# Moving four feature sums, and three products that read them, within layer four of a graph network

## The chip, the cores and the metric

The kernel runs on one core of a Trainium2 chip. Its time is the device time of one launch in microseconds (us). A core has five engines that run their own queues of instructions in order, and wait for one another by semaphores: TensorE (in the profile PE; its weight loads PEld) multiplies matrices into PSUM, VectorE (DVE) and ScalarE (ACT) work element by element, GpSimd (POOL) does so more slowly, and SyncE (SP) issues the DMAs that move data between HBM and SBUF.

## The reference, cut to what matters

There are 16 graphs, each with 1024 nodes of 128 features and a dense 1024 x 1024 adjacency. First comes a small graph network with a layer norm, then a network of four layers with a layer norm:

```
x = layernorm(x + L0(x, adj))          # one aggregation over adj, one linear map, relu
x = layernorm(x + L1(x, adj))          # four layers:
def _layer(nodes, adj, ...):
    src_agg = einsum('bjv,bij->biv', nodes @ ws + bs, l2norm(adj, 2))
    dst_agg = einsum('bjv,bji->biv', nodes @ wd + bd, l2norm(adj, 1))
    self_rep = nodes @ wn + bn
    return tanh(concatenate([src_agg, self_rep, dst_agg]) @ wu + bu)
```

Layers one and two read the output of the layer before. Layers three and four read it together with earlier outputs: layer four reads the outputs of layers three, two and the network's input, 384 features a node. Everything is float32.

## The kernel before, in words

**Folding.** The matrices of a layer are folded, so that a layer is: messages (a linear map of the node features, one part for each direction of the adjacency, SRC and DST), the product of the messages with the scaled adjacency `a` and its scaled transpose `at`, an own part (a linear map of the node's own features), and tanh. Features lie with the feature on the partitions: `f1T` (layer one's output), `f23T` (layer two's, later layer three's), `x_T` (the network's input, also called x1T).

**Seven products instead of eight.** The product of messages and adjacency is done as a 2 x 2 block product in the manner of Strassen and Winograd, so that it takes seven products of quarters. VectorE makes the sums of messages that this needs, S2 to S4 (lines 660 to 663), and the sums of quarters of the adjacency, T2 to T4 for `a` and Q2 to Q4 for `at` (helper `combine`, lines 628 to 632). The products are called M1, M2, M3, M4, Z11, Z12 and Z21; M1 to M4 go to PSUM banks of their own (A, Bk, Dk, Ck), and the Z ones straight to the output halves Z0 and Z1. In layers three and four the own part is done in the same way with the same seven names: its "quarters" are the halves of two feature tensors, in layer four `f1T` and `x_T`. The sums of these quarters are `feature_sums`, four subtractions on VectorE (L798 to L801); in layer four they are made in place. Three of the own products, M1, Z11 and Z12, read the features as they were before; M2, M3, M4 and Z21 read the sums.

**Steps.** A product of 128 x 64 weights fills half of TensorE's columns, so two of them run at once: `upper` and `lower` are two lists of products, and `in_turn` issues them alternately. A step is one entry of `upper` beside one of `lower`, each in two passes; the own product of M3 is cut into two halves of half a step. In layer four there are 34 steps. All engines but SyncE run in the order in which the program is written; SyncE's order comes from the compiler's scheduler. What other engines do during a layer is placed by step: `events` (inside `aggregate`: the sums, and the reads of PSUM, `m1_read` to `last_reads`) and `hooks` (work for other graphs) are dictionaries from an upper step to a function, which is called ahead of that step; at one step the event goes ahead of the hook.

**What lies around the change.** While layer four of graph b runs, the hooks do the first layer norm of graph n = b + 1 and prepare its adjacency:

- step 0, `squares0`: the sum v of squares (L400)
- step 7, `rstd0`: a small product pv on TensorE, ve from it on VectorE (L408), the power -1/2 on GpSimd (L410, output rs), and then `combine(4)`, the subtraction L632 that makes the quarter sum T4 of graph b again (`T_again`), since the first network of graph n had used its place
- step 14, `end0`: the features times rs (L415), and their transposes into the place of `x_T` (L450)
- step 18, `quarters0`: T2 and T3 of graph n (L628, L630); steps 23 and 27: the transposes of its rows into `at` (L605), from row loads (`rows`, `rows_xa`, `rows_acc`) that ScalarE has scaled (L597)

Then layer one of graph n begins: its messages (L206), the additions of the bias to them (L648), their sums S (L660 to L663), and its 30 steps. Its hook at step 0 makes the last transposes, from `rows`, `rows_xa` and `rows_acc`. This is so for 15 of the graphs; the last has no next one.

Of the kernel before, what the change touches and what calls it, by code (L numbers as in the profile page):

```python
# [23 lines left out]
def adj_resnorm_kernel(ctx: ExitStack, tc: tile.TileContext, x, adj, w0, b0, layers, out):  # L24
# [44 lines left out]
    NJ = NB // 2  # L69

    def blocks(ap):

        return ap.rearrange("p (k g c) -> p g k c", g=G, c=C)
# [5 lines left out]
    def half(h):  # L79
        return slice(h * HW, (h + 1) * HW)  # L80
# [127 lines left out]
    def product(name, i=None):  # L208
        if i is None:
            return ps_t.tile([P, HW], F32, tag="pt", name=name)  # L210
        return ps_p.tile([P, HW], F32, tag=f"p{i}", name=name)
# [422 lines left out]
    SRC, DST = 0, 1  # L634
# [58 lines left out]
    def aggregate(b, l, feats, msgs, wm, a, at, T, Q, fT, etag, hooks={}, pieces=1, sums=None):  # L693
# [5 lines left out]
        Z0, Z1 = (product(f"z{h}_{l}_{b}", h) for h in range(NH))  # L699

        Ck = product(f"m4_{l}_{b}")
        Dk = product(f"m3_{l}_{b}")
        A, Bk = (product(f"m{i}_{l}_{b}") for i in (1, 2))
# [4 lines left out]
        def own(v, h, chosen=feats):  # L708
            return [(own_weights(wm, l, c)[:, v * V:(v + 1) * V], blocks(f[:, half(h)])) for f, c in chosen]

        def prod(name, part):
            y, t = Y[part], TT[part]
            x, y = {"M1": lambda: (X[0, 0], y[0, 0]), "M2": lambda: (S[2], t[2]), "M3": lambda: (S[3], t[3]),
                    "M4": lambda: (S[1], y[0, 1]), "Z11": lambda: (X[0, 1], y[1, 0]),
                    "Z12": lambda: (S[4], y[1, 1]), "Z21": lambda: (X[1, 1], t[4])}[name]()
            return [(x[:, k, part], y[:, k]) for k in range(NJ)]
# [3 lines left out]
        def m1_read():  # L720
            nc.scalar.copy(e0[high], A[high])  # L721
            nc.scalar.copy(e0[low], A[high])

        def m4_read():
            nc.scalar.copy(e2[high], Ck[low])
            nc.scalar.copy(e2[low], Ck[low])
# [15 lines left out]
        def m3_half():  # L742
            nc.scalar.copy(e1[high], Dk[low])

        def m2_and_half_of_m3():
            m2_read()
            nc.vector.tensor_add(e0[high], e0[high], e1[high])
# [6 lines left out]
        if l == 0:  # L754
            upper = [
                (Z1, True, own(1, 1)), (Z0, True, own(1, 0)),
                (A, True, prod("M1", DST)), (Bk, True, prod("M2", DST)), (A, False, prod("M1", SRC)),
                (Z0, False, prod("Z21", DST)), (Bk, False, prod("M2", SRC)), (A, True, prod("M3", SRC)),
                (Z0, False, prod("Z21", SRC)),
            ]  # L760
            lower = [
                (Z1, True, own(0, 1)), (Z0, True, own(0, 0)),
                (Dk, True, prod("M3", DST)), (Ck, True, prod("M4", DST)), (Z1, False, prod("Z12", DST)),
                (Z0, False, prod("Z11", DST)), (Ck, False, prod("M4", SRC)), (Z1, False, prod("Z12", SRC)),
                (Z0, False, prod("Z11", SRC)),
            ]

            def m4_and_m2_read():
                m4_read()
                m2_and_half_of_m3()  # L770

            events = {10: m3_half, 14: m1_read, 22: m4_and_m2_read, 26: last_reads}
        elif l == 1:
            upper = [
                (Z1, True, own(1, 1)), (Z0, True, own(1, 0)),
                (A, True, prod("M1", DST) + prod("M1", SRC)), (Bk, True, prod("M2", DST) + prod("M2", SRC)),
                (A, True, prod("M3", SRC)), (Z0, False, prod("Z21", DST)), (Z0, False, prod("Z21", SRC)),
            ]
            lower = [
                (Z1, True, own(0, 1)), (Z0, True, own(0, 0)),  # L780
                (Dk, True, prod("M3", DST)), (Ck, True, prod("M4", DST) + prod("M4", SRC)),
                (Z1, False, prod("Z12", SRC) + prod("Z12", DST)),
                (Z0, False, prod("Z11", SRC) + prod("Z11", DST)),
            ]

            def first_reads():
                m1_read()
                m3_half()

            events = {10: first_reads, 14: m4_read, 18: m2_and_half_of_m3, 22: last_reads}  # L790
        else:
            f0, f1 = (next(f for f, c in feats if c == k) for k in PAIRED[l])
            rest = [(f, c) for f, c in feats if c not in PAIRED[l]]
            y = {(j, h): f[:, half(h)] for j, f in enumerate((f0, f1)) for h in range(NH)}
            y4, y3 = (y[0, 1], y[0, 0]) if sums is None else sums

            def feature_sums():
                nc.vector.tensor_sub(y4, y[0, 1], y[0, 0])  # L798
                nc.vector.tensor_sub(y[1, 1], y[1, 1], y4)
                nc.vector.tensor_sub(y3, y[1, 1], y[0, 0])  # L800
                nc.vector.tensor_sub(y[1, 0], y[1, 0], y[1, 1])  # L801

            def w(at):
                return wx[l][:, at:at + V]

            own_of = {"M1": (w(0), y[0, 0]), "M2": (w(S2W), y[1, 1]), "M3": (w(S3W), y3), "M4": (w(S1W), y4),
                      "Z11": (w(P), y[1, 0]), "Z12": (w(S4W), y[1, 1]), "Z21": (w(P + V), y[1, 0])}

            def of_own(name, *gs):
                x, f = own_of[name]  # L810
                return [(x, blocks(f), *gs)]

            m3, m3s = prod("M3", DST), prod("M3", SRC)
            lower_m3 = of_own("M3", slice(0, G // 2)) + m3[NJ - 1:]
            upper_m3 = m3s[:NJ - 1] + of_own("M3", slice(G // 2, G)) + m3s[NJ - 1:]
            m4 = prod("M4", DST) + prod("M4", SRC) + of_own("M4")
            z12 = prod("Z12", SRC) + prod("Z12", DST)
            if l < NL - 1:
                z11 = prod("Z11", SRC) + prod("Z11", DST)
                upper = [  # L820
                    (A, True, of_own("M1") + prod("M1", DST) + prod("M1", SRC)),
                    (Bk, True, prod("M2", DST) + prod("M2", SRC) + of_own("M2")), (A, True, upper_m3),
                    (Z0, True, prod("Z21", DST) + prod("Z21", SRC) + of_own("Z21")),
                ]
                lower = [
                    (Z1, True, of_own("Z12")), (Z0, True, of_own("Z11") + z11[:2]), (Dk, True, m3[:NJ - 1]),
                    (Ck, True, m4), (Dk, False, lower_m3), (Z1, False, z12), (Z0, False, z11[2:]),
                ]

                def m3_half_and_m2_read():  # L830
                    m3_half()
                    m2_and_half_of_m3()

                events = {2: feature_sums, 9: m1_read, 16: m4_read, 18: m3_half_and_m2_read, 23: m3_read, 26: second_half}
            else:
                upper = [
                    (Z1, True, own(1, 1, rest)), (Z0, True, own(1, 0, rest)),
                    (A, True, of_own("M1") + prod("M1", DST) + prod("M1", SRC)),
                    (Z0, False, of_own("Z21")),
                    (Bk, True, of_own("M2") + prod("M2", DST) + prod("M2", SRC)), (A, True, upper_m3),  # L840
                    (Z0, False, prod("Z21", SRC) + prod("Z21", DST)),
                ]
                lower = [
                    (Z1, True, own(0, 1, rest)), (Z0, True, own(0, 0, rest)),
                    (Z1, False, of_own("Z12")), (Z0, False, of_own("Z11")),
                    (Ck, True, m4), (Dk, True, m3[:NJ - 1] + lower_m3),
                    (Z1, False, z12), (Z0, False, prod("Z11", SRC) + prod("Z11", DST)),
                ]
                events = {4: feature_sums, 11: m1_read, 13: m4_read, 17: m3_half, 21: m2_and_half_of_m3, 26: last_reads}

        for i, (o, x, y_, start, stop) in in_turn(flat_steps(upper, high), flat_steps(lower, low)):
            if i in events:
# [235 lines left out]
    for b in range(B):  # L1088
# [64 lines left out]
        else:  # L1153
# [23 lines left out]
            def first_addition(st=st):  # L1177
                if nxt:
                    add_squares(n, st, 1)

            hooks = {0: rows3, 3: weights1, 5: lambda: combine_1(yt), 7: lambda: combine(2, yt, Q),
                     9: lambda: combine(3, yt, Q), 11: lambda: combine(4, yt, Q), 17: sums1, 28: first_addition}
            aggregate(b, 0, feats, t, wm, a, at, T, Q, f1, "row", hooks)
            wm = ahead["wm"]
            a2, xs2 = w.get("a"), None
# [125 lines left out]

        hooks = alongside(hooks, {23: weights3})
        aggregate(b, 2, feats, t, wm, a, at, T, Q, f23, "acc", hooks, sums=(sums[:, half(0)], sums[:, half(1)]))
        wm = ahead["wm"]
        if nxt:
# [155 lines left out]
```

## Time and profile before

| | us |
|---|---|
| median of 3 runs | 2455.91 (2451.87 to 2457.41) |
| span of the profiled run | 2450.8 |
| TensorE busy | 2418.3 (99%) |
| VectorE busy | 1988.7 (81%) |
| ScalarE busy | 957.9 (39%) |
| GpSimd busy | 274.0 (11%) |
| from graph to graph | about 150 |

In lines of the timeline the columns are start, duration, engine, source line, operation, output <- inputs, shapes and count; in brackets, the idle time of the engine ahead of it and what ended that. A group of several instructions has one line, from the first start to the last end. In a list of waits the numbers are the total, the count and the longest. A matmul's duration is modelled and overlaps the next one's: two passes of one half start 0.43 us apart, though each is shown as 0.59. The granted clock of TensorE was 0.999 of full speed.

### The profile page before, as it was taken

What the parts mean: (1) busy time and instruction counts of PE and PEld (TensorE: products, weight loads), DVE (VectorE), ACT (ScalarE), POOL (GpSimd) and SP (SyncE); (2) the same over time, 40 slices, a digit from 0 to 9 for tenths busy, and PEclk for the clock granted to TensorE, in tenths of its full rate; (3) what the DMA queues carried; (4) which work ended last, traced back from release to release, by engine and by line L of the source; (5) the groups of instructions that cost most, each with busy time, mean ns of one, the idle gap of its engine ahead of it and who ended that gap; (6) DMA issues with size and microseconds to landing.
All of it is one profiled execution on the core that took longest, in us unless ns stands there. A gap on an engine that the chain in (4) does not pass through costs nothing.

```text
span 2450.8 us, 34735 instructions
## 1 busy us (share of the span) xinstructions
PE 2418.3 (99%) x13245; PEld 1032.5 (42%) x13245; DVE 1988.7 (81%) x2631; ACT 957.9 (39%) x1795; POOL 274.0 (11%) x102
## 2 busy tenths in 40 slices
PE   8999999999999999999999999999999999999998
PEld 4444344443434444443443434434444344433433
DVE  5988878798787988879788788887888878798753
ACT  5415334253342624426143351533525334252311
POOL 4101111101111011110011110111100111101100
PEclk9999999999999999999999999999999999999999
DMA  9517254361634517245172452724436254351400
GB/s 206 110 53 146 53 114 93 74 126 44 136 72 91 108 44 157 52 99 104 47 157 59 83 107 62 139 59 101 93 75 133 47 124 84 81 117 44 97 16 18
DMA packets 365733, 222.09 MB, mean 91 GB/s; under 512 B 152769, under 2 KB 336833, under 8 KB 365569
## 3 DMA queue, kind: packets, MB, share of 16 engines
q1 hardware_dynamic: 364800, 217.53, 41.7%
q0 software_dynamic: 768, 2.36, 0.4%
q8 instruction: 105, 1.72, 0.3%
q14 instruction: 60, 0.48, 0.1%
HBM read 201.20 MB, written 18.60 MB: 90 GB/s over the span
## 4 chain that ended last, share of the span: by engine, by line
PE 80%; DVE 9%; DMA 5%; issue 2%; POOL 2%; SPq 1%; ACT 1%; DVEq 0%; POOLq 0%; ACTq 0%
PE m L856 37%; PE z L856 18%; PE pt L206 15%; PE m_f L537 5%; PE z_f L537 2%; PE pw L206 2%; DMA a<-in_adj_dram 2%; POOL rs L410 2%; DVE at L605 2%; DMA rows_acc<-in_adj_dram 1%; SPq L590 1%; DVE at L624 1%; DVE Q L628 1%; DVE T L632 1%; DVE T L628 1%
## 5 line engine op out<-in xcount | busy, mean ns | idle before, releaser
L856 PE MATMUL m<-Q,S 128*64 128x512 f32 x1008 | 453.2, 593 | 1.5 <-DVE Q L628 1.2
L856 PE MATMUL m<-a,t 128*64 128x512 f32 x1008 | 415.0, 595 | 9.4 <-DVE t L648 9.4
L856 PE MATMUL m<-at,t 128*64 128x512 f32 x1008 | 411.3, 595 | 2.7 <-DVE at L605 2.7
L410 POOL TENSOR_TENSOR rs<-ve,mhalf 128x32 f32<-128x32 f32 x30 | 191.6, 6386 | 1965.7 <-DVE ve L408 1965.7
L856 PE MATMUL m<-T,S 128*64 128x512 f32 x1008 | 394.8, 593 | 1.2
L648 DVE TENSOR_TENSOR t<-pt,wm 128x512 f32<-128x512 f32 x256 | 170.5, 684 | 135.1 <-PE pt L206 135.1
L856 PEld LDWEIGHTS m<-Q,S 128*64 128x64 f32 x1008 | 135.6, 137 | 256.3 <-issue 237.0
L856 PE MATMUL z<-at,t 128*64 128x512 f32 x504 | 229.2, 592 | 0.0
L856 PE MATMUL z<-a,S 128*64 128x512 f32 x504 | 227.3, 594 | 0.0
L856 PE MATMUL z<-a,t 128*64 128x512 f32 x504 | 226.8, 592 | 0.0
L856 PE MATMUL z<-at,S 128*64 128x512 f32 x504 | 226.7, 592 | 0.0
L856 PE MATMUL z<-Q,t 128*64 128x512 f32 x504 | 226.6, 592 | 0.0
L206 PE MATMUL pt<-wm,f1T 128*64 128x256 f32 x1536 | 214.3, 382 | 2.5 <-ACT f1T L869 2.5
L721 ACT COPY e<-m 64x512 f32<-64x512 f32 x63 | 36.6, 581 | 403.4 <-PE m L856 403.0
L856 PEld LDWEIGHTS m<-a,t 128*64 128x64 f32 x1008 | 124.2, 137 | 158.2 <-issue 124.4
L856 PEld LDWEIGHTS m<-T,S 128*64 128x64 f32 x1008 | 123.1, 137 | 128.0 <-issue 124.6
L856 PEld LDWEIGHTS m<-at,t 128*64 128x64 f32 x1008 | 124.9, 137 | 123.8 <-issue 109.5
L856 PE MATMUL z<-T,t 128*64 128x512 f32 x384 | 172.8, 592 | 0.0
L276 ACT ACTIVATE sq<-a 128x1024 f32<-128x1024 f32 x120 | 125.9, 1049 | 77.4 <-DVE acc L285 63.3
L368 DVE TENSOR_TENSOR a<-a,cinv 128x512 f32<-128x512 f32 x250 | 154.1, 693 | 0.7 <-DMA cinv<-dr 0.7
L206 PE MATMUL pt<-wm,f23T 128*64 128x256 f32 x1024 | 154.0, 379 | 0.0
L206 PE MATMUL pt<-wm,x_T 128*64 128x256 f32 x1024 | 136.1, 379 | 0.0
(264 smaller groups left out, 4428.9 us busy)
## 6 DMA issues: line engine op xcount, KB each, us to landing
a<-in_adj_dram SPq DMA_DIRECT2D x120, 512.0 KB, 11.2
a<-in_adj_dram SPq DMA_DIRECT2D x240, 128.0 KB, 4.4
rows<-in_adj_dram SPq DMA_DIRECT2D x240, 64.0 KB, 3.0
wm<-wsave SPq DMA_DIRECT2D x31, 320.0 KB, 3.9
wm<-wsave SPq DMA_DIRECT2D x16, 512.0 KB, 6.3
xn<-in_x_dram SPq DMA_DIRECT2D x124, 64.0 KB, 1.9
xs<-in_x_dram SPq DMA_DIRECT2D x60, 128.0 KB, 3.5
cinv<-dr SPq DMA_DIRECT2D x30, 256.0 KB, 5.1
```

Source lines behind the costliest of these rows:

```text
L206: nc.tensor.matmul(out[s], x[:, s], y, start=start, stop=stop)
L276: nc.scalar.activation(sq, a[:, i, :], AF.Square, accum_out=state["cols"][:, i:i + 1])
L368: engine.tensor_mul(a[:, i, s], a[:, i, s], cinv[:, s])
L410: nc.gpsimd.tensor_tensor(rstd, ve, mhalf[:, :n], ALU.pow)
L537: nc.tensor.matmul(o, x_, y_, start=start, stop=stop)
L590: queue.dma_start(piece[g * C:(g + 1) * C, :, h * P:(h + 1) * P], v[h, g, :, i * n:(i + 1) * n])
L605: nc.vector.transpose(at[h][:, j:j + NJ, c].rearrange("p j (k c) -> p j k c", c=C), piece.rearrange("p k (j c) -> p j k c", c=C)[:, j:j + NJ])
L624: nc.vector.tensor_sub(y[0, 1], y[0, 1], y[0, 0])
L628: nc.vector.tensor_sub(T[2], y[1, 1], y[0, 1])
L648: nc.vector.tensor_add(t[j][:, o:o + 2].rearrange("p k a v c -> p k (a v c)"), pt, wm[:, 0][:, None, :].to_broadcast([P, 2, 2 * P]))
L721: nc.scalar.copy(e0[high], A[high])
L856: nc.tensor.matmul(o, x, y_, start=start, stop=stop)
```

## The change

Only layer four is touched. `feature_sums` goes from ahead of step 4 to ahead of step 8, which puts the four sums behind the hook of step 7 in VectorE's order: behind ve and behind the subtraction L632. The own products that read the sums go some steps later in TensorE's order: M2 from step 12 to step 15, into the middle of the message products of M2; Z21 from step 11 to step 16; M4, on the lower half, from step 12 to step 15, behind the first three message products of M3. The reads of M4 and of half of M3 from PSUM (`m4_read`, `m3_half`) follow, from steps 13 and 17 to 16 and 18. No product, sum or load is added or taken away. It is for a better order on VectorE during the layer norm of the next graph.

```diff
@@ layer four (l == NL - 1) @@
                 upper = [
                     (Z1, True, own(1, 1, rest)), (Z0, True, own(1, 0, rest)),
                     (A, True, of_own("M1") + prod("M1", DST) + prod("M1", SRC)),
-                    (Z0, False, of_own("Z21")),
-                    (Bk, True, of_own("M2") + prod("M2", DST) + prod("M2", SRC)), (A, True, upper_m3),
+                    (Bk, True, prod("M2", DST) + of_own("M2")), (Z0, False, of_own("Z21")),
+                    (Bk, False, prod("M2", SRC)), (A, True, upper_m3),
                     (Z0, False, prod("Z21", SRC) + prod("Z21", DST)),
                 ]
                 lower = [
                     (Z1, True, own(0, 1, rest)), (Z0, True, own(0, 0, rest)),
                     (Z1, False, of_own("Z12")), (Z0, False, of_own("Z11")),
-                    (Ck, True, m4), (Dk, True, m3[:NJ - 1] + lower_m3),
+                    (Ck, True, m4[:-1]), (Dk, True, m3[:NJ - 1]), (Ck, False, m4[-1:]), (Dk, False, lower_m3),
                     (Z1, False, z12), (Z0, False, prod("Z11", SRC) + prod("Z11", DST)),
                 ]
-                events = {4: feature_sums, 11: m1_read, 13: m4_read, 17: m3_half, 21: m2_and_half_of_m3, 26: last_reads}
+                events = {8: feature_sums, 11: m1_read, 16: m4_read, 18: m3_half, 21: m2_and_half_of_m3, 26: last_reads}
```

## The prediction

> **What bounds the kernel now.** I read the busy times first. TensorE is busy 99% of the span, so a gain can come only from moments in which it waits or runs half full. VectorE follows at 81%, and GpSimd is nearly empty, which will matter all the same.
>
> ```profile
> PE 2418.3 (99%) x13245; PEld 1032.5 (42%) x13245; DVE 1988.7 (81%) x2631; ACT 957.9 (39%) x1795; POOL 274.0 (11%) x102
> ```
>
> Next the waits of TensorE. One recurs once per pair of graphs: 15 times, always 0.6 us, for the message additions (L648), and it falls in layer one of the next graph.
>
> ```profile
> PE m L856 <- DVE t L648: 9.4, 15, 0.6
> PE m L856 <- DVE at L605: 2.7, 2, 1.7
> ```
>
> That figure understates the loss, since the two halves of the array run apart: when one half waits and the other works, the trace shows no idle time. So I took stages. These are layer four of graph 6, layer one of graph 7 and layer two of graph 7 (counting from 0). Layers one and two do the same 30 steps with the same shapes.
>
> ```profile
> 1076.00:1104.90 28.90, 28.90 (x146) 12.52 (x144) 22.19 (x25) 11.29 (x24) 7.39 (x2) 1.00 0.78 159
> 1104.90:1136.60 31.70, 30.79 (x154) 11.94 (x152) 29.79 (x33) 17.45 (x35) 0.00 (x0) 1.00 0.78 160
> 1136.60:1166.20 29.60, 29.60 (x168) 11.28 (x164) 25.48 (x30) 19.43 (x34) 5.43 (x1) 1.00 0.23 49
> ```
>
> The first two numbers are the length and TensorE's busy time, the fourth group VectorE's. Layer one takes 2.1 us more than layer two, which even holds a few small extra products; without stalls layer one would be 3.46 (messages) + 30 x 0.857 = 29.2 us, so about 2.5 us are lost there. And VectorE is busy 29.79 of those 31.70 us: layer one is bound by VectorE, which arrives late. The timeline at the boundary shows how late:
>
> ```profile
> 1106.13 2.36 DVE L605 STREAM_TRANSPOSE at<-a 128x1024 f32<-128x1024 f32 x2
> 1108.42 0.65 DVE L858 TENSOR_TENSOR e<-e,z 128x512 f32<-128x512 f32 x1
> 1108.99 2.47 DVE L648 TENSOR_TENSOR t<-pt,wm 128x512 f32<-128x512 f32 x4
> 1111.49 0.76 DVE L660 TENSOR_TENSOR S<-t 128x256 f32<-128x256 f32 x2
> ...
> 1110.92 1.07 PE L856 MATMUL m<-a,t 128*64 128x512 f32 x2 [0.63 <-DVE t L648]
> 1112.07 0.61 PE L856 MATMUL m<-T,S 128*64 128x512 f32 x1
> ```
>
> TensorE had begun the layer's own products at 1108.36; two steps later, at 1108.36 + 1.72 = 1110.08, both halves could have begun the message products. The upper half began at 1110.92 and the lower, which needs S3, at 1112.07: 2.0 us late. Whatever makes VectorE earlier here by up to 2.0 us is gained in full.
>
> Why is VectorE late? Going back through its order from 1111.5 there is no idle time above 0.7 us until this, in layer four:
>
> ```profile
> 1081.85 0.68 DVE L798 TENSOR_TENSOR f1T<-f1T 128x512 f32<-128x512 f32 x1
> 1082.63 0.69 DVE L799 TENSOR_TENSOR x_T<-x_T,f1T 128x512 f32<-128x512 f32 x1
> 1083.36 0.69 DVE L800 TENSOR_TENSOR f1T<-x_T,f1T 128x512 f32<-128x512 f32 x1
> 1083.97 0.68 DVE L801 TENSOR_TENSOR x_T<-x_T 128x512 f32<-128x512 f32 x1
> 1084.57 0.18 DVE L408 TENSOR_SCALAR ve<-pv 128x32 f32<-128x32 f32 x1
> 1084.67 2.28 DVE L632 TENSOR_TENSOR T_again<-a,T 128x2048 f32<-128x2048 f32 x1
> 1092.27 1.23 DVE L415 TENSOR_TENSOR y<-y,rs 128x1024 f32<-128x1024 f32 x1 [5.32 <-POOL inv L263]
> ```
>
> VectorE stands 5.32 us before L415. The releaser named is a memset behind the power on GpSimd; what it needs is the power itself (rs, L410), and that could not start before ve (L408), queued behind the four feature sums.
>
> **What the Trainium skill says.** "SBUF — State Buffer", section Who interferes with whom: a VectorE instruction with two SBUF inputs contends with a GpSimd instruction that reads SBUF, and the second to issue waits for the first. The trace agrees. The power takes 5.43 us in layer two, and 7.34 in layer four, where the big subtraction L632, with two SBUF inputs, has just begun:
>
> ```profile
> 1008.94 5.43 POOL L410 TENSOR_TENSOR rs<-ve,mhalf 128x32 f32<-128x32 f32 x1 [67.94 <-DVE ve L408]
> 1084.90 7.34 POOL L410 TENSOR_TENSOR rs<-ve,mhalf 128x32 f32<-128x32 f32 x1 [64.46 <-DVE ve L408]
> 1092.19 0.10 POOL L263 MEMSET inv<- 128x8 f32 x1
> ```
>
> 1092.24 - 5.43 = 1086.81, and L632 ends at 1086.95: the power in effect runs from the end of that subtraction. "Perfetto Trace Analysis", section GPSIMD Engine Instruction, warns that a GpSimd span is unreliable; here its end is confirmed by the start of L415 right behind it.
>
> **The change part by part.** No instruction is added or removed; three things move.
>
> *The sums behind the subtraction.* VectorE's order was v, four sums, ve, L632; it becomes v, ve, L632, four sums. ve needs TensorE's product pv, which ran at 1082.04 for 0.30 us, so ve can start at about 1082.4 in place of 1084.57: 2.17 us earlier. L632 then runs from 1082.5 to 1084.8, the power in effect from 1084.65 for 5.43 us to 1090.1, and L415 begins there: again 2.1 to 2.2 us earlier. The sums take 2.80 us as a block and run 1084.8 to 1087.6, in what was idle time. VectorE then waits about 2.5 us instead of 5.3.
>
> *Do the own products wait for the sums?* A step of TensorE (both halves, two passes) is 0.86 us. Step 7 started at 1082.13, behind pv. The M2 and M4 own products go to step 15: 1082.13 + 8 x 0.86 = 1089.0. They need the first two sums, done by 1086.3. The Z21 own product is at step 16, 1089.9, and needs the last, done at 1087.6. At least 2.2 us of slack; before, the slack was 0.9 (sums done 1084.65, read at 1085.59). Cost on TensorE: nothing, hidden behind the M2 and M4 message products moved ahead.
>
> *Later readers and buffers.* The Z21 own product now ends near 1090.9, and the next graph's features (L450) overwrite its input from 1091.4: 0.5 us to spare. T2's last reader moves two steps earlier, T3's stays. ScalarE's M4 copies move three steps later, to about 1090, where it was idle.
>
> *How far the 2.15 us travel.* From L415 to L648 VectorE waits only 0.68 us, for a ScalarE copy that itself follows VectorE. PSUM inputs are ready long before: M2 by 1094.4 against its read at 1099.51, M3 by 1098.2 against 1104.00, Z0 by 1105.2 against 1108.42. So L648 would start near 1106.85, its fourth addition ends at 1109.3 (its product ends at 1108.6), S3's first half at 1109.7 and the lower half starts at its unstalled 1110.1. Further on, the transposes of the last rows need a load, and this chain must shift too:
>
> ```profile
> 1108.64 0.31 SPq L219 DMA_DIRECT2D a<-in_adj_dram  x1
> 1109.04 5.04 SPq L590 DMA_DIRECT2D rows_acc<-in_adj_dram  x8
> ...
> 1118.22 1.31 DVE L605 STREAM_TRANSPOSE at<-rows_acc 128x512 f32<-128x512 f32 x2 [0.20 <-ACT rows_acc L597]
> ```
>
> The first adjacency load starts 0.15 us after the transposes that free its buffer (1108.49), and the row loads are queued behind it. Both hang on VectorE and so come 2.15 us earlier. Without that, the transposes would end where they do now, and so would everything behind them. Behind them, the Q sum (L628) is the last wait of the layer, and it moves with VectorE's order.
>
> Sum: 2.1 us for each of 15 boundaries (the last graph has no next one, and its sums have ample time) is 31.5 us: 2455.9 - 31.5 = 2424.4.
>
> **Unknown, bounded.** Does the waiting power get the port between L632 and the first sum, or only after the last? In the first graph GpSimd and VectorE both run multiplications L368; a GpSimd one issued at 59.35 took 1.46 us, and a VectorE one queued behind another at 59.60 took 1.76 in place of 0.69. They alternate, so the waiting power should get its turn at once: lower bound 0. Upper bound: it waits out the sums and starts at 1087.5. I take 0. Does the power then hold up the sums? In layer two L285, with two SBUF inputs, ran at its normal 1.22 us 0.11 us into a power. I take 0 there too; the upper bound is that they wait the full 5.43 us.
>
> **Rivals.**
> - *Part of the shift is lost* on the way, in the row loads or a wait that shows only now: half of it, 1.05 x 15 = 16, gives 2440. For it: four engines and a load chain must all move together. Against: none of them showed slack that was used up.
> - *No change*: the row loads stay where they are, say because their queue is ordered otherwise. The transposes end at 1118.9 as before and layer one is as long: 2456. For it: that queue isn't in the program's written order. Against: its head is released by VectorE.
> - *Slower, by the port*: the power starts behind the sums and ends at 1092.9, 0.7 us later than now; x 15 = 10, 2466. If instead the sums waited for the whole power, they would end at 1092.9 and step 16 would stall 3 us per graph: 2501. Against: the two observations above.
>
> **How the numbers follow.** Forecast 0.62 (2419 to 2429), partial 0.15, no change 0.07, slower 0.16 with other stalls on the moved products. The likeliest gives 2424.4. The low end is the whole loss of layer one regained, 2.5 x 15 = 37.5, 2418, less a little for the scatter of the runs (2451.87 to 2457.41): 2416. Upwards I go past the partial case, to 2448. Faster by over 0.2%: 0.62 + 0.15 = 0.77; within: 0.06; slower: 0.17.
>
> **What would show it.** Right: ve before the sums, the idle time before L415 near 2.5 us, the power still 7.3 us long, the waits for L648 gone, layer one near 29.6 us, layer four still 28.9. Wrong: a longer power or a sum far above 0.69 us (port); a TensorE wait for L798 to L801 (slack misjudged); row transposes waiting longer for ScalarE (loads).

## The result, and the profile after

The changed kernel takes 2423.4 us (median of 4 runs, 2421.63 to 2425.39) against 2454.5 (now also of 4 runs, 2451.87 to 2457.41): a ratio of 0.9873, with a 95% interval of 0.9856 to 0.9890. The forecast was 2424.4.

The three stages of the kernel after, for the same graphs as before (layer four of graph 6, layers one and two of graph 7):

```profile
1063.10:1092.00 28.90, 28.90 (x146) 12.51 (x144) 24.43 (x27) 12.62 (x26) 7.39 (x2) 1.00 0.78 157
1092.00:1121.26 29.26, 29.26 (x155) 13.12 (x153) 27.66 (x31) 16.11 (x33) 0.00 (x0) 1.00 0.86 173
1121.26:1150.80 29.54, 29.54 (x166) 11.25 (x164) 25.46 (x30) 19.43 (x34) 5.43 (x1) 1.00 0.24 49
```

Layer four, the only one whose program changed, takes 28.90 us as before. The gain is in layer one of the next graph: 29.26 us in place of 31.70, with TensorE busy all the time. Graph 7 is one of the better ones. Taken from the first product of the messages (L206) to that of the next layer, layer one took 31.41 to 32.84 us before, and 33.54 in the last graph; now it takes 29.25 or 29.26 in four graphs, 29.33 to 31.31 in ten, and 33.86 in the last. Over all 15 that is 451.0 us in place of 476.3: 25.3 of the 27.3 us by which the spans of the two profiled runs differ.

The cause lies in layer four all the same, in the timeline of VectorE. (The layer reads the outputs of layers three and one and the network's input, not that of layer two; `f1T` is layer one's.)

```profile
1069.47 0.19 DVE L408 TENSOR_SCALAR ve<-pv 128x32 f32<-128x32 f32 x1 [0.45 <-PE pv L206]
1069.58 2.28 DVE L632 TENSOR_TENSOR T_again<-a,T 128x2048 f32<-128x2048 f32 x1
1071.78 0.74 DVE L798 TENSOR_TENSOR f1T<-f1T 128x512 f32<-128x512 f32 x1
1072.56 0.69 DVE L799 TENSOR_TENSOR x_T<-x_T,f1T 128x512 f32<-128x512 f32 x1
1073.28 0.69 DVE L800 TENSOR_TENSOR f1T<-x_T,f1T 128x512 f32<-128x512 f32 x1
1073.89 0.68 DVE L801 TENSOR_TENSOR x_T<-x_T 128x512 f32<-128x512 f32 x1
1077.18 1.23 DVE L415 TENSOR_TENSOR y<-y,rs 128x1024 f32<-128x1024 f32 x1 [2.61 <-POOL inv L263]
```

The sums stand where VectorE was idle, and the idle time before L415 fell from 5.32 to 2.61 us. The power on GpSimd lasts as long as before, 2.2 us earlier against TensorE's step 7 (1069.22 here, 1082.13 before):

```profile
1069.81 7.34 POOL L410 TENSOR_TENSOR rs<-ve,mhalf 128x32 f32<-128x32 f32 x1 [62.29 <-DVE ve L408]
```

At the boundary the additions start 1.90 us behind the first product that makes the messages (L206, 1092.00; from here on "behind the first message product" counts from it), where it was 4.08. Both halves of TensorE begin the products of messages and adjacency at once, 1.72 us behind the layer's own ones (1095.45):

```profile
1093.90 2.49 DVE L648 TENSOR_TENSOR t<-pt,wm 128x512 f32<-128x512 f32 x4
...
1097.17 0.59 PE L856 MATMUL m<-a,t 128*64 128x512 f32 x1
1097.22 0.59 PE L856 MATMUL m<-T,S 128*64 128x512 f32 x1
```

In the list of TensorE's waits the 15 for L648 are gone. The waits for row transposes (L605), which need the rows that ScalarE has scaled (L597), have grown from 2.7 us at two boundaries to 6.2 at four:

```profile
PE m L856 <- DVE at L605: 6.2, 4, 2.9
PE m L856 <- DVE Q L628: 1.0, 5, 0.2
```

### The profile page after: what moved, and what is told of

It is laid out like the page before. It is cut to its first block, busy times and chain, and to the rows that moved or that the text cites. A ratio compares the mean times of both kernels' runs of the same rounds, so it can differ in the third digit from the quotient of the medians.

```text
span 2423.5 us, 34721 instructions
## 1 busy us (share of the span) xinstructions
PE 2399.2 (99%) x13245; PEld 1027.6 (42%) x13245; DVE 1991.4 (82%) x2631; ACT 957.8 (40%) x1795; POOL 274.1 (11%) x102
## 3 DMA queue, kind: packets, MB, share of 16 engines
q8 instruction: 105, 1.72, 0.3%
## 4 chain that ended last, share of the span: by engine, by line
PE 85%; DMA 6%; DVE 5%; SPq 2%; issue 2%; ACT 1%; DVEq 0%; POOLq 0%; ACTq 0%
PE m L856 40%; PE z L856 19%; PE pt L206 15%; PE m_f L537 5%; DMA a<-in_adj_dram 3%; PE z_f L537 2%; PE pw L206 2%; SPq L590 1%; DVE at L605 1%; DMA rows_acc<-in_adj_dram 1%; DVE at L624 1%; DVE Q L628 1%; DVE T L632 1%; DMA rows<-in_adj_dram 1%; DMA raw<-in_L_gnn_ws_dram 1%
## 5 line engine op out<-in xcount | busy, mean ns | idle before, releaser
L856 PE MATMUL m<-T,S 128*64 128x512 f32 x1008 | 415.4, 593 | 0.0
L856 PE MATMUL m<-a,t 128*64 128x512 f32 x1008 | 409.4, 593 | 0.0
L648 DVE TENSOR_TENSOR t<-pt,wm 128x512 f32<-128x512 f32 x256 | 170.7, 685 | 133.2 <-PE pt L206 133.2
L206 PE MATMUL pt<-wm,f1T 128*64 128x256 f32 x1536 | 213.2, 380 | 2.5 <-ACT f1T L869 2.5
L368 DVE TENSOR_TENSOR a<-a,cinv 128x512 f32<-128x512 f32 x250 | 154.2, 693 | 1.3 <-DMA cinv<-dr 1.3
L206 PE MATMUL pt<-wm,f23T 128*64 128x256 f32 x1024 | 154.0, 379 | 0.0
L206 PE MATMUL pt<-wm,x_T 128*64 128x256 f32 x1024 | 136.1, 379 | 0.0
## 6 DMA issues: line engine op xcount, KB each, us to landing
a<-in_adj_dram SPq DMA_DIRECT2D x120, 512.0 KB, 10.7
```

The costliest lines, as they stand in the source:

```text
L206: nc.tensor.matmul(out[s], x[:, s], y, start=start, stop=stop)
L368: engine.tensor_mul(a[:, i, s], a[:, i, s], cinv[:, s])
L648: nc.vector.tensor_add(t[j][:, o:o + 2].rearrange("p k a v c -> p k (a v c)"), pt, wm[:, 0][:, None, :].to_broadcast([P, 2, 2 * P]))
L856: nc.tensor.matmul(o, x, y_, start=start, stop=stop)
```

## The experiments

Theory A: the gain comes from VectorE's order, by way of an earlier power. Theory B: it comes from TensorE's new order of own products.

**One half of the change at a time.** First the products alone, with the sums ahead of step 4 as before:

```diff
-events = {8: feature_sums, 11: m1_read, 16: m4_read, ...}
+events = {4: feature_sums, 11: m1_read, 16: m4_read, ...}
```

> The own products in their new places, the sums ahead of step 4 as before. Theory A (the gain is VectorE's order: ve and the power start 2.2 us earlier): nothing gained, 2450 to 2458 us; ve about 2.4 us behind the start of step 7, the 5.3 us of idle time before L415 and the waits for L648 are back. Theory B (the gain is TensorE's order of products): 2424 us, as in the changed kernel.

Measured: 2454.6 us, ratio to before 1.0001 (0.9992 to 1.0009). In the timeline of VectorE the old idle time is back:

```profile
1095.15 1.23 DVE L415 TENSOR_TENSOR y<-y,rs 128x1024 f32<-128x1024 f32 x1 [5.32 <-POOL inv L263]
```

The waits for L648 are back too, 9.3 us in 15. The new order of products alone is worth nothing. Then the sums alone, in the kernel before:

```diff
-events = {4: feature_sums, 11: m1_read, 13: m4_read, ...}
+events = {8: feature_sums, 11: m1_read, 13: m4_read, ...}
```

> The sums behind the subtraction, the own products in their old places. Theory A: VectorE keeps its 2.2 us, but the Z21 own product at step 11, 3.46 us behind step 7, waits for the last sum, which ends 5.35 us behind it: 1.9 us lost in layer four of each of 15 graphs, 28 us, less up to 0.3 us a graph in layer one, where VectorE now leads by more. Layer four near 30.8 us, layer one 29.2 to 29.6, in all 2445 to 2455 us. Theory B (the products' order makes the gain): without it layer one stays at 31.7 us and layer four grows, 2470 to 2484 us.

Measured: 2447.8 us, ratio 0.9976 (0.9967 to 0.9985). TensorE's waits and its timeline at step 11:

```profile
PE z L856 <- DVE x_T L801: 26.0, 15, 1.7
```
```profile
1084.89 0.64 PE L856 MATMUL z<-x_T,wx 128*64 128x512 f32 x1 [1.73 <-DVE x_T L801]
```

The Z21 own product waits for the last sum (L801) in each of 15 graphs. From the messages of layer four to those of layer one it is 41.35 us in place of 39.35, and layer one takes 29.21. So VectorE's lead is there, and TensorE pays 2.0 us a graph for it in layer four. Theory B has fallen: the moved products give nothing by themselves; they only give the sums the time to come late.

**Is it the port that makes the power long?** In the changed kernel L632 was put behind the four sums, by a hook of its own at step 8:

```diff
-def rstd0(w=w, y=y, T=T):
+def rstd0(w=w):
     w["r"] = norm_rstd(w["v"], KS, nm)
+def quarter_sum0(y=y, T=T):
     combine(4, y, T)
-hooks = {0: squares0, 7: rstd0, 10: rows0, ...}
+hooks = {0: squares0, 7: rstd0, 8: quarter_sum0, 10: rows0, ...}
```

> The changed kernel with one more swap on VectorE: ve, the four sums, and only then the subtraction L632. Port theory (the power waits for the VectorE instruction that runs when it is issued): it now waits for a sum of 0.69 us in place of a subtraction of 2.28, so its duration falls from 7.34 to about 5.8 us and L415 could start 1.6 us earlier; but L450 then overwrites the input of the Z21 own product, which ends 8.8 us behind step 7, so only about 0.5 us of that reaches layer one: 2418 to 2424 us. If the power were simply slower in layer four, it stays at 7.3 us and the time at 2423.

Measured: 2419.8 us, ratio 0.9863 (0.9848 to 0.9877). The power, and VectorE around L415:

```profile
1067.57 5.74 POOL L410 TENSOR_TENSOR rs<-ve,mhalf 128x32 f32<-128x32 f32 x1 [62.29 <-DVE ve L408]
```
```profile
1070.00 2.28 DVE L632 TENSOR_TENSOR T_again<-a,T 128x2048 f32<-128x2048 f32 x1
1073.35 1.23 DVE L415 TENSOR_TENSOR y<-y,rs 128x1024 f32<-128x1024 f32 x1 [1.06 <-POOL inv L263]
1075.80 1.30 DVE L450 STREAM_TRANSPOSE x_T<-y 128x512 f32<-128x512 f32 x2 [1.23 <-PE z L856]
```

The same power on the same data is 1.60 us shorter because a shorter instruction runs when it is issued: 2.28 - 0.68 = 1.60. So its extra time is a wait for VectorE's running instruction. That shows the wait, not the port: both instructions have two SBUF inputs, and no run has one with a single input in their place. And the next limit shows as expected: L450 now waits 1.23 us for the Z21 own product, whose input it overwrites.

The own products in their old places take that wait away, and with the sums right behind ve they can go there. Against the kernel just told of:

```diff
-(Bk, True, prod("M2", DST) + of_own("M2")), (Z0, False, of_own("Z21")),
-(Bk, False, prod("M2", SRC)), (A, True, upper_m3),
+(Z0, False, of_own("Z21")),
+(Bk, True, of_own("M2") + prod("M2", DST) + prod("M2", SRC)), (A, True, upper_m3),
...
-(Ck, True, m4[:-1]), (Dk, True, m3[:NJ - 1]), (Ck, False, m4[-1:]), (Dk, False, lower_m3),
+(Ck, True, m4), (Dk, True, m3[:NJ - 1] + lower_m3),
...
-events = {8: feature_sums, 11: m1_read, 16: m4_read, 18: m3_half, ...}
+events = {8: feature_sums, 11: m1_read, 13: m4_read, 17: m3_half, ...}
```

> VectorE: ve, the sums, the subtraction; the own products in their old places. The sums end 3.2 us behind step 7, just ahead of the Z21 own product at 3.46, so TensorE should not wait; the power again near 5.8 us; the readers of the old features end early, so L450 is free and VectorE gains 1.6 us on the changed kernel. Layer one then has only its waits for row loads and Q left, some 0.3 us a graph and 6 us at four boundaries: 2412 to 2420 us. If TensorE does wait for a sum, by up to 0.3 us a graph, the gain is gone: 2423. Theory B: back at 2455, since the products are in their old places.

Measured: 2418.3 us, ratio 0.9859 (0.9844 to 0.9874). L450 no longer waits, and the additions start 1.11 us behind the first message product, held now by the products themselves. Layer one takes 29.25 us in all graphs but the last, where the changed kernel has that in four. Below 29.25 the further lead saves nothing. What it comes with is that the rows are no longer late, so that the waits for row transposes are gone, except the last graph's.

**The same work ahead of the wait and behind it.** An extra sum over 128x1024 on VectorE, read by nothing, ahead of L415 or right behind it:

```diff
 def end0(w=w):
+    extra = two.tile(...)   # in both kernels, ahead of its sum
+    nc.vector.reduce_sum(extra, w["ys"][:, KS], axis=AX.X)   # first kernel
     norm_end(w["ys"], w["r"], KS)
+    nc.vector.reduce_sum(extra, w["ys"][:, KS], axis=AX.X)   # second kernel
```

> The changed kernel with one more VectorE instruction per graph, a sum over 128x1024 of about 1.22 us whose result nothing reads, ahead of L415, where VectorE stands idle for 2.6 us. Theory A: hidden in full, 2420 to 2426 us. If any added work on VectorE cost its time, 2441.

> The same instruction right behind L415. Theory A (whatever makes VectorE later between L415 and layer one's additions comes back in TensorE's time nearly in full): 1.1 to 1.22 us for each of 15 graphs, 2438 to 2443 us, and the waits for L648 return. If VectorE's lateness there were harmless, 2423 as for the instruction ahead of L415.

Measured, on a chip where the kernel before took 2449.8 us: 2419.4 us ahead of L415, ratio 0.9877 (0.9862 to 0.9892), which is the changed kernel's own; and 2432.6 behind it, ratio 0.9932 (0.9918 to 0.9945). Ahead, the idle time takes it up. Behind, it costs 13.2 us; VectorE and TensorE at the boundary of that kernel, where the messages had begun at 1094.88:

```profile
1097.83 2.47 DVE L648 TENSOR_TENSOR t<-pt,wm 128x512 f32<-128x512 f32 x4
```
```profile
1100.05 1.02 PE L856 MATMUL m<-a,t 128*64 128x512 f32 x2
1100.91 0.61 PE L856 MATMUL m<-T,S 128*64 128x512 f32 x1
```

The additions start 2.95 us behind the messages, 1.05 later than in the changed kernel, and layer one takes 30.27 us, 1.01 more. The lower half starts 0.86 us late, though none of it shows as idle time of TensorE, since the upper half is at work; the waits for L648 that were expected back are there for TensorE's weight loads alone. The expected 2438 to 2443 us was missed, for the most part because the kernel before took 4.7 us less here than beside the first runs. Two sizes were off too. The instruction costs 1.05 us rather than 1.22, because it and its neighbours follow one another more closely than L415 and L450 did. And 13.2 us is 0.88 a graph; in layer one of all 15 graphs the two profiled runs differ by 15.3 us, or 1.02 a graph, and the rest of the second run was 1.4 us shorter.

Put together, the delay of the additions sets the length of layer one where nothing else is late (the shortest of the 15), down to what TensorE itself needs. The totals hold more than that:

| kernel | additions behind first message product, us | shortest layer one, us | all 15, us |
|---|---|---|---|
| before | 4.08 | 31.41 | 476.3 |
| products alone | 4.07 | 31.39 | 480.2 |
| changed, extra sum behind L415 | 2.95 | 30.27 | 458.4 |
| changed | 1.90 | 29.25 | 451.0 |
| changed, extra sum ahead of L415 | 1.89 | 29.25 | 443.1 |
| ve, sums, L632 | 1.41 | 29.25 | 443.6 |
| the same, old products | 1.11 | 29.24 | 443.3 |

The rest of the span lies between 1972.4 and 1974.5 us in all seven, so what tells these kernels apart is in layer one. What sets the remaining graphs is when ScalarE begins on the last rows (L597, `rows_acc`). In graph 7 of the changed kernel that is 9.03 us behind the first message product:

```profile
1101.03 1.71 ACT L597 ACTIVATE rows_acc<-rows_acc,rinv 128x256 f32<-128x256 f32 x4 [3.74 <-DMA rows_acc<-in_adj_dram]
```

In its ten graphs of 29.33 to 31.31 us these rows come at 9.19 to 11.16, and layer one is 20.15 us longer than that number, to 0.01, whether TensorE shows a wait or not. Over all 180 layer ones of the twelve profiled runs, 170 are the longest of three, to 0.05 us: 29.25, the additions' delay plus 27.33, and the rows' delay plus 20.15. The two constants are fitted to these runs. The other ten, seven of them in the last graph, are 1.05 to 1.32 us longer. In the changed kernel all three nearly meet, so a little lateness of either kind shows.

**The waits that are left.** The last 16 row loads went to GpSimd's queue:

```diff
 rows[0] = load_rows(n, 0, [one.tile(...)
-                           for tag in ("xa", "acc")])
+                           for tag in ("xa", "acc")], nc.gpsimd)
```

> The changed kernel with the last 16 row loads of each graph (rows_xa, rows_acc) issued by GpSimd in place of SyncE, so that they no longer stand behind the first adjacency load. If the waits for the row transposes that are left in layer one (6.2 us at four boundaries, and up to 0.3 us of VectorE waiting at others) come from that queue, they go: 2412 to 2420 us. If they come from the bandwidth of the loads, nothing changes: 2423. If GpSimd is too slow in issuing, VectorE waits longer for the scaled rows: 2430 or more.

> The row loads on GpSimd, with VectorE's order of ve, sums, subtraction and the products in their old places. If both what is left on VectorE and what is left in the load queue bind in layer one, the two add up: 2406 to 2416 us. If one hides the other, no better than the better one of the two alone.

Measured: 2424.2 us, ratio 0.9898 (0.9885 to 0.9912), and 2440.7, ratio 0.9968 (0.9955 to 0.9980) with VectorE's other order, on the chip on which the extra sum ahead of L415 gave 2419.4. Neither expected gain came. The graphs differ, though. At 12 of 15 boundaries of the first kernel all eight loads of `rows_acc` were issued ahead of the first of the eight adjacency loads of 512 KB (the last graph has none), ScalarE had the rows 5.2 to 6.8 us behind the first message product, and layer one took 29.25 or 29.26 us. So here, at the boundary to graph 6 (first message product at 942.20):

```profile
939.39 4.32 POOL L590 DMA_DIRECT2D rows_acc<-in_adj_dram  x8 [7.70 <-ACT a L597]
947.38 1.70 ACT L597 ACTIVATE rows_acc<-rows_acc,rinv 128x256 f32<-128x256 f32 x4
```

Such early rows gain little, for most came in time already; but the last graph's wait is gone (29.26 us, where the kernel with the extra sum ahead of L415 had 33.19). At the three others the last row load went out behind one, two and seven adjacency loads, the rows came at 9.5, 10.3 and 15.4, and layer one took 29.67, 30.45 and 36.91: more than the last graph gained. This is the last of them (graph 7, first message product at 1089.90, adjacency loads issued from 1091.45 to 1095.25):

```profile
1088.06 0.55 POOL L590 DMA_DIRECT2D rows_acc<-in_adj_dram  x1 [8.67 <-DVE e L733]
1091.20 3.79 POOL L590 DMA_DIRECT2D rows_acc<-in_adj_dram  x7 [2.59 <-issue]
```
```profile
1105.35 1.70 ACT L597 ACTIVATE rows_acc<-rows_acc,rinv 128x256 f32<-128x256 f32 x4 [10.17 <-DMA rows_acc<-in_adj_dram]
```

Why GpSimd paused for 2.59 us stays open; the other 14 groups of eight have no such pause. In the combination VectorE's lead brings the adjacency loads forward, to 0.29 us behind the first message product from 1.55, and not GpSimd's row loads. At 12 boundaries three to eight adjacency loads are out before the last row load, the rows come at 9.6 to 14.8, and layer one takes 29.77 to 36.10 us. At the two others that have such loads, with one ahead, the rows come by 6.5 and layer one takes 29.25. So an earlier issue does bring the rows earlier, as long as they stay ahead of the adjacency loads, or nearly so. That these loads slow the rows fits the order of issue at every boundary of the two kernels, but no kernel that holds them back was tried.

**Side by side once more**, the changed kernel and the version with the sums right behind ve and the old products:

> The changed kernel once more, beside the next one on one chip. If the waits for row transposes at three boundaries, beside the last, came with this order of VectorE, they are there again (about 6 us in four waits); if they were a matter of one run's load times, they fall elsewhere or are gone. Ratio to the kernel before 0.986 to 0.989.

> ve, sums, subtraction, with the products in their old places, once more. Layer one is already at TensorE's own 29.25 us at the ordinary boundaries of the changed kernel, so VectorE's further 1.5 us can only shorten the few late ones: 2 to 5 us less than the changed kernel. If VectorE's lead counted everywhere, 20 us less.

Measured: 2422.7 us, ratio 0.9875 (0.9861 to 0.9890), and 2418.8, ratio 0.9858 (0.9842 to 0.9875). In the changed kernel two of the three extra waits for row transposes fell in other graphs this time, for 6.4 us in four with the last; the other version had only the last graph's, 2.5 us (2.7 in its first run). So these waits come and go with the times of the loads. Over all 15 layer ones the two profiled runs took 451.3 and 443.2 us, and the rows of the other version came by 8.63 us in all graphs but the last, early enough by the fit above. That VectorE's further lead does this is likely, since the row loads are queued behind an adjacency load that VectorE releases, 0.29 us behind the first message product in place of 1.56. But the kernel with the extra sum ahead of L415, without that lead, had late rows in three graphs only, beside a kernel before that was 4 us faster. The 3.9 us between the medians fits the expected 2 to 5, and all four runs of the other version (2417.59 to 2420.05) lie below all four of the changed kernel (2420.95 to 2427.06); but the intervals of the ratios overlap: it is likely the better kernel, not shown to be.

## Why the prediction was right

- **VectorE's order.** ve was to start 2.17 us earlier; against step 7 it is 2.19 (2.44 us behind it before, 0.25 now). The idle time before L415 was to be 2.5, and is 2.61.
- **The port.** The lower bound was taken, that the waiting power gets its turn between L632 and the first sum. It ran 7.34 us as before; had it waited for all sums it would have been over 10. The sums were not held up beyond 0.06 us in the first. That the wait is for VectorE's running instruction was an inference from one comparison; the swap of L632 and the sums showed it (5.74 us). That the second to issue waits for the first holds here one way only: VectorE's sums L799 to L801 ran beside the power at 0.68 to 0.69 us, as without it.
- **Slack of the own products.** None was seen to wait, and from the messages of layer four to those of layer one it is 39.35 us in every graph, as before. That the slack had to be made by moving them is shown by the sums alone, where TensorE lost 2.0 us a graph, 1.9 expected.
- **Buffers.** The spare 0.5 us ahead of L450 was read rightly: L415 1.6 us earlier met a wait of 1.23.
- **Travel to layer one.** The additions were to start 1.94 us behind the first message product (1106.85 - 1104.91); they start 1.90 behind it. The load chain moved with VectorE: the first adjacency load is issued at 1093.56, 0.15 us behind the transposes. Its landings did not move alike: at four boundaries the rows still came at 10.6 us or later. Of the 2.5 us that the forecast saw lost at graph 7, the additions alone make 2.16 (31.41 less 29.25); that graph's late rows, at 11.57 us, make the rest.
- **The sum** was 2.1 x 15 = 31.5 us; the medians differ by 31.1, or 2.07 a boundary. That it comes so near is in part luck. The boundaries are not alike: where rows were late neither before nor after, the gain was 2.16 us; at graph 7, where they were late before alone, 2.46; at four others, where they were late after, 1.65 or less; and at the last nothing (33.54 before, 33.86 after). In the two profiled runs this makes 25.3 us, 1.69 a boundary. The medians are 3.8 us further apart than these runs' spans, and have no trace that would tell why. The forecast had left such losses to the partial rival. And the lead of 2.18 us happens to match the loss of 2.16: a further lead (1.41, 1.11) gained nothing there, and with 1.05 us less of it layer one was 1.02 us longer.

## What to carry to other kernels

On an in-order engine, put what a slow engine is waiting for ahead of work with slack, so that this work fills the wait; and move the readers of that work along, or the gain is paid back there. A stall need not be where its cause is: here layer one waited for an order of work 24 us earlier in layer four, and going back along the late engine to its last long idle time found it. When two halves of an engine run apart, compare the lengths of stages with like work, since a half that waits beside one that works leaves no idle time in the trace. And compare all repeats of a stage, not one: here one graph in the changed kernel looked free of waits, while ten others were held by late rows.

## What the runs showed of the hardware

- A power on GpSimd, issued while VectorE ran an instruction with two SBUF inputs, began when that one ended, even if another followed directly: 7.34 us behind a subtraction of 2.28, 5.74 behind one of 0.68, 5.43 with none. VectorE paid little for giving way: L798 took 0.74 us (median) in place of 0.68, and its later instructions with two SBUF inputs ran beside the power at their usual length (L799 0.69, L285 1.22). Other GpSimd instructions do hold VectorE up: beside a multiplication L368 over 128x512 in the first graph, VectorE's own L368 took 1.76 us in place of 0.69.
- Loads of 64 KB issued by GpSimd took 0.548 us each to issue. Those of `rows_acc` landed in 2.3 us in the median and in 10.7 at most, behind seven adjacency loads; in the changed kernel, issued by SyncE and mostly behind one adjacency load, they took 4.4 in the median.
